# Graph attention, then multi-head attention over 64 graphs: the first batch's order, where weight sums are made, and the one-time checks

## The chip, the cores and the metric

The kernel runs on one core of a Trainium2 chip. The metric is the device time of one execution in microseconds; the median of several runs is compared. Engines are named as in the profile: PE is TensorE (PEld its weight loads), DVE is VectorE, ACT is ScalarE, POOL is GpSimd, SP is the engine that issues most DMAs.

## The reference

There are 64 graphs of 256 nodes with 512 features each, one adjacency matrix for all, and everything is float32.

```python
# layer 0
h = jnp.maximum(_layernorm(x, axis=-1), 0.0)
Wh = jnp.einsum('bnd,de->bne', h, W)
logits = (Wh @ a_src)[:, :, None] + (Wh @ a_dst)[:, None, :]
logits = jnp.where(logits >= 0, logits, 0.2 * logits)      # then -inf where adj == 0
x = x + jnp.einsum('bnm,bmd->bnd', jax.nn.softmax(logits, axis=-1), Wh)
# layer 1
h = jnp.maximum(_layernorm(x, axis=-1), 0.0)
q, k, v = (split_heads(h @ w.T + b) for w, b in ((Wq, bq), (Wk, bk), (Wv, bv)))   # 8 heads of 64
scores = jnp.einsum('bhqd,bhkd->bhqk', q, k) / 8.0         # then -inf where adj == 0
out = jnp.einsum('bhqk,bhkd->bhqd', jax.nn.softmax(scores, axis=-1), v)
x = x + out.transpose(0, 2, 1, 3).reshape(b, n, 512) @ Wo.T + bo
```

## The kernel before, in words

One batch (one graph, two tiles of 128 nodes) is one unit g. Each stage of a batch is a Python generator: `normalize0` (layer norm, ReLU, and the two row sums es and ed against W a_src and W a_dst, L514), `weights0` (exponentials of the logits on ACT, maximum on DVE, mask and sum, L540 to L545), `aggregate0` (h times the edge weights), `transform0` (times W, added to x), `normalize1`, `transpose1`, `project_qk`, `project_v`, `attention`, `scale`, `output`. The lists `first_half` and `second_half` say by hand, for every iteration i, which stage of which batch makes its next step, so a step that stands in the lists is issued at that place on every engine it uses. [...]

Big weight products are made by a seven-product scheme: a 2x2 block product with 7 instead of 8 block products. It needs sums of the left operand's quarters (`combine`: us for layer 0, hs for q, k and v, as for the output) and of the weights' quarters. `load_quarters` puts four quarters of a weight in slots B11, B21, B22 and T3; `combine_w` makes T1 and T2 (part 0), then overwrites T3 and writes T4N (part 1). T3 holds the upper right quarter until then. Before the change, all weight sums are on DVE (L158 to L162); `combine` is on DVE for batch 0 and on POOL for later ones (L170).

Batch 0 has no seven-product scheme in layer 0: it aggregates first (h times em, L575), then multiplies by W (L622) and adds to x with a scale by row (L628). While batch 0's first sums are made, `busy(12)` issues twelve transposes whose result nobody reads.

Layer 1's softmax is made without a maximum. `constants` is a generator that proves, on the chip, that this is safe: Gram matrices of each head's rows of Wq and Wk (`pgram`, L378, four groups), their squares and fourth powers (`squared`, L392), row sums of the absolute values (L408), squares of the bias rows (L424), of W a (L418) and of Wv (L438). If the check fails, a flag starts `general()`, a slower path, after the rest. `aside()` makes its next step; the prologue and, later, every fourth step of an iteration call it. The upper right quarter of each weight, which part 1 of `combine_w` overwrites, is loaded a second time for it:

```python
def load_b12(src, nm):
    b12 = work.tile([P, DC // 2, HD], F32, tag="b12", name=f"b12_{nm}", bufs=2)
    nc.gpsimd.dma_start(b12, quarter_of(src, 0, 1))
    return b12
```

`output_bias` makes bv @ Wo.T on PE (L333, eight products) and adds it to bo on DVE (L340); `bias_rows` then adds the row to x on POOL (L836).

[...]

Of the kernel before, what the change touches and what calls it, by code (L numbers as in the profile page):

```python
# [16 lines left out]
P = 128  # L17
# [11 lines left out]
def kernel(  # L29
# [102 lines left out]
    def bounded():  # L132
# [23 lines left out]
        def combine_w(wt, parts=(0, 1)):  # L156
            if 0 in parts:
                nc.vector.tensor_sub(wt[:, T1], wt[:, T3], wt[:, B11])  # L158
                nc.vector.tensor_sub(wt[:, T2], wt[:, B22], wt[:, T1])
            if 1 in parts:  # L160
                nc.vector.tensor_sub(wt[:, T3], wt[:, B22], wt[:, T3])
                nc.vector.tensor_sub(wt[:, T4N], wt[:, B21], wt[:, T2])  # L162
# [4 lines left out]
        def combine(a, s, g):  # L167


            engine = nc.gpsimd if g else nc.vector  # L170
            engine.tensor_tensor(s[:, 0], a(1, 0), a(1, 1), op=ALU.add)
            engine.tensor_tensor(s[:, 1], s[:, 0], a(0, 0), op=ALU.subtract)  # L172
            engine.tensor_tensor(s[:, 2], a(0, 0), a(1, 0), op=ALU.subtract)
            engine.tensor_tensor(s[:, 3], a(0, 1), s[:, 1], op=ALU.subtract)
# [61 lines left out]
        def load_b12(src, nm):  # L236

            b12 = work.tile([P, DC // 2, HD], F32, tag="b12", name=f"b12_{nm}", bufs=2)
            nc.gpsimd.dma_start(b12, quarter_of(src, 0, 1))
            return b12  # L240

# [12 lines left out]
        nc.gpsimd.dma_start(adj_sb, adj.rearrange("(c p) m -> p c m", p=P))  # L254
# [6 lines left out]
        wo_sb = load_quarters(woT, "wo_sb")  # L261
        for nm, src in (("bq", bq), ("bk", bk), ("bv", bv)):
            load_col(cols[nm], src)
# [5 lines left out]
        def node_weights():  # L269


# [5 lines left out]
            for c in range(DC):  # L277
                if c == DC // 2:
                    edge_mask()
                for j in range(2):  # L280
# [8 lines left out]
                    )  # L289
            return pas  # L290

        def edge_mask():
            adj_f = work.tile([P, NC, N], F32, tag="em", name="adj_f")
# [29 lines left out]
        def whole(wt, b12):  # L323
            return ((wt[:, B11], b12), (wt[:, B21], wt[:, B22]))

        def output_bias():

            wo_q = whole(wo_sb, load_b12(woT, "o"))
            yield
            pb = bank([P, D], "pbias")  # L330
            for j in range(2):
                for c in range(DC):
                    nc.tensor.matmul(  # L333
                        pb[:, j * HD : (j + 1) * HD],
                        cols["bv"][:, c : c + 1].to_broadcast([P, P]),
                        wo_q[c // 2][j][:, c % 2, :],
                        start=(c == 0),
                        stop=(c == DC - 1),
                    )
            nc.vector.tensor_add(bo_b, pb, bo_b)  # L340
            yield
# [13 lines left out]
        def constants():  # L355
# [8 lines left out]
            load_row(bo_b, bo)  # L364
            b12s = [load_b12(src, nm) for src, nm in ((wqT, "q"), (wkT, "k"))]
            yield
            for n in range(2):
                w_q = whole((wq_sb, wk_sb)[n], b12s[n])

                gm = work.tile([P, DC, DH], F32, tag="gram", name=f"gram_{n}", bufs=2)  # L370
                for pair in range(2):
# [13 lines left out]

                def squared(gm, power):
                    pgs = [bank([P, DC, DH], f"pgram{power}_{n}_{r}") for r in range(2)]
                    for e in range(DC):
                        for r in range(2):
                            half_p = slice(r * DH, (r + 1) * DH)  # L390
                            part = gm[half_p, e, :]
                            nc.tensor.matmul(pgs[r][half_p, e, :], part, part, start=True, stop=True)  # L392
                    return pgs

                pgs = squared(gm, 2)
                yield
                gm = work.tile([P, DC, DH], F32, tag="gram", name=f"gram2_{n}", bufs=2)
                for r in range(2):
                    half_p = slice(r * DH, (r + 1) * DH)
                    nc.scalar.copy(gm[half_p], pgs[r][half_p])  # L400
                yield
                pgs = squared(gm, 4)
# [10 lines left out]
            nc.vector.tensor_scalar(ok[:, 0 : 2 * DC], rows, 0.66, None, op0=ALU.is_le)  # L413
            junk = work.tile([P, D], F32, tag="junk", name="junk_b")
            sq = weights.tile([P, 4], F32, tag="sq", name="sq")
            nc.vector.memset(sq, 0.0)
            for j in range(2):
                nc.vector.scalar_tensor_tensor(  # L418
                    junk, wa[j], 1.0, wa[j], op0=ALU.mult, op1=ALU.mult, accum_out=sq[:, j : j + 1]
                )  # L420
            for j, src in enumerate((bq, bk)):
                row = work.tile([1, D], F32, tag="b12", name=f"brow_{j}", bufs=2)
                nc.gpsimd.dma_start(row, src.rearrange("(o e) -> o e", o=1))
                nc.vector.scalar_tensor_tensor(  # L424
                    junk[0:1, :], row, 1.0, row, op0=ALU.mult, op1=ALU.mult,
                    accum_out=sq[0:1, 2 + j : 3 + j],
                )
            nc.vector.tensor_scalar(ok[:, 2 * DC : 2 * DC + 2], sq[:, 0:2], 1.95, None, op0=ALU.is_le)
            nc.vector.tensor_scalar(ok[:, 2 * DC + 2 : 2 * DC + 4], sq[:, 2:4], 1.0, None, op0=ALU.is_le)
            yield  # L430
            big_v = weights.tile([P, 1], F32, tag="big_v", name="big_v")
            wv_q = whole(wv_sb, load_b12(wvT, "v"))
            svs = weights.tile([P, 2 * DC], F32, tag="svs", name="svs")
            for c in range(DC):
                for j in range(2):
                    sqv = work.tile([P, HD], F32, tag="junk", name=f"sqv_{c}_{j}")
                    wc = wv_q[c // 2][j][:, c % 2, :]
                    nc.vector.scalar_tensor_tensor(  # L438
                        sqv, wc, 1.0, wc, op0=ALU.mult, op1=ALU.mult,
                        accum_out=svs[:, 2 * c + j : 2 * c + j + 1],  # L440
                    )
                yield
            nc.vector.tensor_reduce(big_v, svs, AX.X, ALU.add)
            nc.vector.tensor_scalar(
                ok[:, 2 * DC + 4 : 2 * DC + 5], big_v, 1.0e8, None, op0=ALU.is_le
# [46 lines left out]
        def normalize0(g):  # L492
# [5 lines left out]
            stats = Stats(xt, h, f"0_{g}")  # L498
            for t in range(NT):
                stats.mean(t)  # L500
            yield
            for t in range(NT):
                stats.squares(t)
            nmr, rstd = stats.close()
            yield
# [60 lines left out]
        def aggregate0(g):  # L566
# [4 lines left out]
            for dp in range(0, DC, 2):  # L571
# [10 lines left out]
                if g == 0:  # L582
                    nc.scalar.copy(uT[:, dp : dp + 2, :], pu)
                else:
                    nc.vector.tensor_mul(
                        uT[:, dp : dp + 2, :], pu, edges[g][1].unsqueeze(1).to_broadcast([P, 2, N])
                    )
# [5 lines left out]
            scaled = edges.pop(g)[1]  # L593
            if g == 0:
                sums0[g] = uT, scaled
            else:
                sums0[g] = a, four_sums("us", g)
                combine(a, sums0[g][1], g)
            yield

# [12 lines left out]
        def transform0(g):  # L613

            a, s = sums0.pop(g)
            if g == 0:

                uT, rs = a, s
                for t in range(NT):
                    po = bank([P, D], f"po0_{g}_{t}")  # L620
                    for c in range(DC):
                        nc.tensor.matmul(  # L622
                            po, uT[:, c, t * P : (t + 1) * P], w_c[c // 2][:, c % 2, :],
                            start=(c == 0), stop=(c == DC - 1),
                        )
                        if c == 1:
                            yield
                    nc.vector.scalar_tensor_tensor(  # L628
                        xts[g][:, t, :], po, rs[:, t : t + 1], xts[g][:, t, :],
                        op0=ALU.mult, op1=ALU.add,  # L630
                    )
                    yield
                return
            yield from products(
                a, s, f"po0_{g}", partial(product_rows, w_sb), partial(add_to_rows, xts[g])
            )
# [27 lines left out]
        def transpose1(g):  # L664
# [13 lines left out]
            combine(a, lefts[g][1], g)  # L678
            yield

        def project_qk(g):
# [12 lines left out]
            def read(n, ps):  # L694
# [6 lines left out]
                elif n == 4:  # L701
# [6 lines left out]
                    return  # L708
                if held:
# [4 lines left out]
            yield from products(a, s, f"pqk_{g}", partial(product_cols, (wq_sb, wk_sb)), read)  # L714
# [124 lines left out]
        def scale(g):  # L839
# [15 lines left out]
            if s is not None:  # L855
                combine(a, s, g)
# [63 lines left out]
        bias = output_bias()  # L920
# [25 lines left out]
        S, E, W0, L1 = (normalize0, 0), (weights0, 0), (transform0, 0), (normalize1, 0)  # L946
        S_1, E_1, U_1, S_2 = (normalize0, 1), (weights0, 1), (aggregate0, 1), (normalize0, 2)
        steps(S, S, S)
        pas = node_weights()
        busy(12)  # L950
# [248 lines left out]
```

## Time and profile before

| what | us |
|---|---|
| median of 3 runs (2881.25 to 2884.21) | 2881.69 |
| profiled execution | 2883.55 |
| its span, first to last instruction | 2881.8 |
| PE busy in the span | 2857.6 |
| DVE, ACT, POOL busy | 2349.5, 1236.1, 1211.4 |

A group row of the profile names the line, the engine, the operation, then output and inputs by the program's names, and the busy time with the mean of one instruction in ns. A timeline row has the start in us, the length, engine, line and operation; in brackets stands how long the engine was idle before it, and what released it. "Lxyz" is the line in the kernel before. Matmuls in float32 appear as two instructions each.

### The profile page before, as it was taken

How to read it: one execution, taken by the hardware profiler on the slowest of the kernel's cores; microseconds unless marked ns; L12 is line 12 of the kernel's file. 1: busy time of each engine (PE TensorE's matmuls, PEld its weight loads, DVE VectorE, ACT ScalarE, POOL GpSimd, SP SyncE). 2: the span in 40 equal slices, each digit the busy share in tenths (PEclk: the TensorE clock that was granted, in tenths of full speed). 3: DMA queues.
4: the chain of work that ended last, by engine and by line, in shares of the span. 5: the costliest groups of instructions: out<-in, count | busy, mean ns of one | idle time of the engine just before them, and what ended most of it. 6: DMA issues, size and time to landing. Idle time of an engine off the chain costs nothing. (4 is left out here: it accounts for less than half of the span.)

```text
span 2881.8 us, 50781 instructions
## 1 busy us (share of the span) xinstructions
PE 2857.6 (99%) x19676; PEld 2471.1 (86%) x19676; DVE 2349.5 (82%) x3664; ACT 1236.1 (43%) x2986; POOL 1211.4 (42%) x1406
## 2 busy tenths in 40 slices
PE   8999999999999999999999999999999999999999
PEld 6788888888888888888888888888888888888886
DVE  7788888888888888888888888888888888888875
ACT  5443444434434444444344344444443443444432
POOL 2345344354454453443544534534435445345331
PEclk9999999999999999999999999999999999999999
DMA  4121222212212212222122122122221221221221
GB/s 143 20 40 33 40 35 33 45 31 37 45 30 38 38 34 41 33 35 45 30 37 45 30 38 37 35 41 33 35 45 30 38 45 30 38 36 35 34 40 29
DMA packets 82939, 111.89 MB, mean 39 GB/s; under 512 B 11652, under 2 KB 48516, under 8 KB 82694
## 3 DMA queue, kind: packets, MB, share of 16 engines
q1 hardware_dynamic: 82054, 107.00, 23.3%
q8 instruction: 158, 2.59, 0.4%
q0 software_dynamic: 640, 1.58, 0.2%
q14 instruction: 87, 0.71, 0.1%
HBM read 42.48 MB, written 33.55 MB: 26 GB/s over the span
## 5 line engine op out<-in xcount | busy, mean ns | idle before, releaser
L611 DVE TENSOR_TENSOR x<-po,x 128x1024 f32<-128x1024 f32 x875 | 595.0, 686 | 214.4 <-PE po L213 207.5
L485 POOL TENSOR_SCALAR ve<-ssq 128x2 f32<-128x2 f32 x128 | 24.6, 192 | 1090.5 <-ACT h L474 846.1
L758 DVE TENSOR_TENSOR ex<-ex,maskT 128x512 f32<-128x512 f32 x512 | 362.1, 748 | 0.0
L753 ACT ACTIVATE ex<-psc 128x512 f32<-128x512 f32 x512 | 257.8, 624 | 95.2 <-PE psc L745 95.2
L778 ACT COPY aT<-pav 128x512 f32<-128x512 f32 x128 | 75.0, 586 | 501.3 <-PE pav L770 470.0
L222 PEld LDWEIGHTS pqk<-hs,wq_sb 128*128 128x128 f32 x2048 | 268.3, 192 | 14.2 <-DVE hs L172 1.3
L222 PE MATMUL pqk<-hs,wq_sb 128*128 128x128 f32 x2048 | 270.2, 275 | 1.1 <-DVE hs L172 1.1
L222 PE MATMUL pqk<-hs,wk_sb 128*128 128x128 f32 x2048 | 270.5, 275 | 0.0
L213 PE MATMUL pv<-wv_sb,hs 128*128 128x256 f32 x1024 | 262.7, 379 | 0.5 <-DVE v L200 0.5
L514 DVE SCALAR_TENSOR_TENSOR junk<-wa,h 128x512 f32<-128x512 f32 x252 | 252.9, 1004 | 10.8
L213 PE MATMUL po<-wo_sb,as 128*128 128x256 f32 x992 | 255.4, 380 | 0.0
L222 PEld LDWEIGHTS pqk<-hs,wk_sb 128*128 128x128 f32 x2048 | 249.3, 192 | 0.0
L213 PE MATMUL po<-w_sb,us 128*128 128x256 f32 x1008 | 248.4, 379 | 0.0
L575 PE MATMUL pu<-em,h 128*128 128x256 f32 x1024 | 243.4, 381 | 1.9 <-DVE em L543 1.9
L745 PE MATMUL psc<-qk 64*128 64x256 f32 x2048 | 240.0, 384 | 1.8 <-DVE qk L207 1.8
L745 PEld LDWEIGHTS psc<-qk 64*128 64x128 f32 x2048 | 194.0, 188 | 48.3 <-issue 24.7
L770 PE MATMUL pav<-ex,v 128*64 128x256 f32 x2048 | 235.4, 382 | 0.0
L704 ACT ACTIVATE p<-pqk,bias 128x128 f32<-128x128 f32 x256 | 73.2, 369 | 353.2 <-PE pqk L222 353.2
L793 DVE RECIPROCAL rc<-psm 128x256 f32<-128x256 f32 x64 | 112.5, 1758 | 132.9 <-PE psm L785 132.9
L575 PEld LDWEIGHTS pu<-em,h 128*128 128x128 f32 x1024 | 195.6, 191 | 28.9 <-issue 2.0
L836 POOL TENSOR_TENSOR x<-x,bo_b 128x512 f32<-128x512 f32 x128 | 217.4, 1718 | 2.6 <-DVE bo_b L340 2.6
L770 PEld LDWEIGHTS pav<-ex,v 128*64 128x64 f32 x2048 | 141.4, 137 | 85.6 <-DVE x L611 19.2
(206 smaller groups left out, 5880.1 us busy)
## 6 DMA issues: line engine op xcount, KB each, us to landing
x<-in_x_dram SPq DMA_DIRECT2D x64, 512.0 KB, 5.6
out_dram<-x SPq DMA_DIRECT2D x128, 256.0 KB, 2.0
rb<-rc SPq DMA_DIRECT2D x496, 64.0 KB, 4.8
wq_sb<-in_L_gnn_Wq_dram SPq DMA_DIRECT2D x4, 256.0 KB, 9.5
wk_sb<-in_L_gnn_Wk_dram SPq DMA_DIRECT2D x4, 256.0 KB, 8.0
w_sb<-in_L_gnn_W_dram SPq DMA_DIRECT2D x4, 256.0 KB, 7.0
wv_sb<-in_L_gnn_Wv_dram SPq DMA_DIRECT2D x4, 256.0 KB, 8.8
wo_sb<-in_L_gnn_Wo_dram SPq DMA_DIRECT2D x4, 256.0 KB, 7.7
```

Of the source, the lines that this page charges most:

```text
L213: nc.tensor.matmul(dst[:, 0:HD], left[:, c, :], wt[:, slot, c, :], start=c == 0, stop=c == 1)
L222: nc.tensor.matmul(dst[:, at : at + P], wt[:, slot, c, e * P : (e + 1) * P], left[:, c, :], start=c == 0, stop=c == 1,)
L514: nc.vector.scalar_tensor_tensor(junk, (wa if g else pas)[a], 1.0, h[:, t, :], op0=ALU.mult, op1=ALU.mult, accum_out=dst[:, t : t + 1],)
L575: nc.tensor.matmul(pu[:, d, :], h[:, m, (dp + d) * P : (dp + d + 1) * P], em[:, m, :], start=(m == 0), stop=(m == NC - 1),)
L611: nc.vector.tensor_add(dst, src, dst)
L745: nc.tensor.matmul(psc[r][:, m, :], qk[rows, 2 + e % 2, m * P : (m + 1) * P], qk[rows, e % 2, :], start=True, stop=True,)
L753: nc.scalar.activation(ex[:, r, :, :], psc[r], AF.Exp, scale=SCALE)
L758: nc.vector.tensor_mul(ex[:, r, :, :], ex[:, r, :, :], maskT)
L770: nc.tensor.matmul(pav[r * DH : (r + 1) * DH, i, :], v[j][:, m, at : at + DH], pair[i][:, r, m, :], start=(m == 0), stop=(m == NC - 1),)
L778: nc.scalar.copy(aT[j], pav)
L793: nc.vector.reciprocal(rc, psm)
L836: nc.gpsimd.tensor_tensor(part, part, bo_b, op=ALU.add)
```

## The change

- Batch 0's layer 0 becomes a stage `layer0`: h is transposed, h @ W is made while the logits are made, and the edge weights are applied to the product. `aggregate0` and `transform0` lose their branch for g = 0.
- `combine_w` takes an engine: wk, w and wv are summed on POOL, wq and wo on DVE. `combine` is on POOL but for batch 0's hs.
- The Gram check stops at the square, with the bound on row sums 1.0 in place of 0.66 on fourth powers. The Gram matrices are made before part 1 of `combine_w` overwrites T3, so the second loads of quarters go. Squares of wv are made by ACT (`value_squares`), those of bq and bk from columns with one small product (`pq`).
- The output bias is made by four DVE steps and one product with a matrix of ones.
- The adjacency and bo are loaded from SP's queue. The mask is made after batch 0's es and ed.
- Batch 1's first layer norm takes its statistics from DVE's bn_stats instead of ACT.
- The prologue's order, iteration 0's lists, and the order of batch 0's seven q/k products are new (0, 2, 1, 3, ...), with product 2 held back for adding.

```diff
-        def combine_w(wt, parts=(0, 1)):
+        def combine_w(wt, engine, parts=(0, 1)):
...
+                    engine.tensor_tensor(wt[:, to], wt[:, a], wt[:, b], op=ALU.subtract)
-        def combine(a, s, g):
-            engine = nc.gpsimd if g else nc.vector
+        def combine(a, s, engine=nc.gpsimd):
...
-        nc.gpsimd.dma_start(adj_sb, adj.rearrange("(c p) m -> p c m", p=P))
+        nc.sync.dma_start(adj_sb, adj.rearrange("(c p) m -> p c m", p=P))
...
+        nc.sync.dma_start(bo_b, bass.AP(tensor=bo.tensor, offset=bo.offset, ap=[[0, P], [1, D]]))
...
                 if c == DC // 2:
-                    edge_mask()
+                    busy(4)
...
+                    if c >= DC // 2:
+                        busy(2)
...
-        def whole(wt, b12):
-            return ((wt[:, B11], b12), (wt[:, B21], wt[:, B22]))
+        def whole(wt):
+            return ((wt[:, B11], wt[:, T3]), (wt[:, B21], wt[:, B22]))
...
         def output_bias():
-            wo_q = whole(wo_sb, load_b12(woT, "o"))
-            yield
+            terms = work.tile([P, 2, HD], F32, tag="junk", name="terms")
+            for c in range(DC):
+                rows = wo_sb[:, B11 : T3 + 1 : T3 - B11] if c < 2 else wo_sb[:, B21 : B22 + 1]
+                part, bv_c = rows[:, :, c % 2, :], cols["bv"][:, c : c + 1]
+                if c == 0:
+                    nc.vector.tensor_scalar(terms, part, bv_c, None, op0=ALU.mult)
+                else:
+                    nc.vector.scalar_tensor_tensor(
+                        terms, part, bv_c, terms, op0=ALU.mult, op1=ALU.add
+                    )
             pb = bank([P, D], "pbias")
-            for j in range(2):
-                for c in range(DC):
-                    nc.tensor.matmul(
-                        pb[:, j * HD : (j + 1) * HD],
-                        cols["bv"][:, c : c + 1].to_broadcast([P, P]),
-                        wo_q[c // 2][j][:, c % 2, :],
...
+            nc.tensor.matmul(pb, ones, terms.rearrange("p j e -> p (j e)"), start=True, stop=True)
             nc.vector.tensor_add(bo_b, pb, bo_b)
+        def value_squares():
+            for n, slot in enumerate((B11, B21, B22, T3)):
+                junk = work.tile([P, DC // 2, HD], F32, tag="ex", name=f"junk_v_{n}", bufs=4)
+                nc.scalar.activation(
+                    junk, wv_sb[:, slot], AF.Square, accum_out=svs[:, n : n + 1]
+                )
...
+            if g == 1:
+                mv, rstd = norm_stats(xt, f"0_{g}", small)
...
+        def layer0(g):
+            h = nodes[g][0]
+            hT = big.tile([P, DC, TOK], F32, tag="uT", name="hT0")
+            for t in range(NT):
+                pt = bank([P, DC, P], f"pt0_{t}")
+                for c in range(DC):
+                    nc.tensor.transpose(pt[:, c, :], h[:, t, c * P : (c + 1) * P], ident)
+                nc.scalar.copy(hT[:, :, t * P : (t + 1) * P], pt)
+                yield
+            hw = big.tile([P, NT, D], F32, tag="qk0", name="hw")
+            for t in range(NT):
+                pw = bank([P, D], f"phw_{t}")
+                for c in range(DC):
+                    nc.tensor.matmul(
+                        pw, hT[:, c, t * P : (t + 1) * P], w_c[c // 2][:, c % 2, :],
+                        start=(c == 0), stop=(c == DC - 1),
+                    )
+                    if c == 1:
+                        yield
+                nc.scalar.copy(hw[:, t, :], pw)
+                yield
+            del nodes[g]
+            em, rs = edges.pop(g)
+            pos = [bank([P, D], f"po0_0_{t}") for t in range(NT)]
+            for m in range(NC):
+                for t in range(NT):
+                    nc.tensor.matmul(
+                        pos[t], em[:, m, t * P : (t + 1) * P], hw[:, m, :],
+                        start=(m == 0), stop=(m == NC - 1),
+                    )
+                    if m:
+                        part = xts[g][:, t, :]
+                        nc.vector.scalar_tensor_tensor(
+                            part, pos[t], rs[:, t : t + 1], part, op0=ALU.mult, op1=ALU.add
+                        )
+                        yield
+                if m == 0:
+                    yield
...
+            order = range(7) if g else (0, 2, 1, 3, 4, 5, 6)
...
         steps(S, S, S)
         pas = node_weights()
-        busy(12)
...
+        steps(S, L0, L0)
+        keep_wa(pas)
+        steps(L0, E)
+        edge_mask()
+        steps(L0, S_1, E, S_1, L0, L0, S_1, E, L0)
+        combine_w(wk_sb, nc.gpsimd, (0,))
+        combine_w(w_sb, nc.gpsimd, (0,))
+        combine_w(wq_sb, nc.vector, (0,))
+        prepare_biases()
+        steps(E_1, L0, L0, L1, E_1)
+        aside(6)
+        combine_w(wq_sb, nc.vector, (1,))
+        steps(L1, E_1, U_1, L1, U_1, X)
         aside(2)
...
+        combine_w(wk_sb, nc.gpsimd, (1,))
+        combine_w(w_sb, nc.gpsimd, (1,))
+        steps(X, X)
-        first = [(load, 3), K, K, E0, K, US, K, E0, K, K, K]
+        first = [(load, 3), K, D0, K, D0, K, US, K, D0, K, D0, K, E0, K, W, E0, W]
...
             if i == 0:
-                todo = first + second_half[:5] + [E0] + second_half[5:]
+                todo = first + [A, A, N0, E0] + second_half[6:]
...
+                if i == 0 and n == 6:
+                    value_squares()
                 if i == 0 and n == 8:
-                    combine_w(w_sb)
-                if i == 0 and n == len(first):
-                    combine_w(wv_sb)
+                    combine_w(wv_sb, nc.gpsimd)
                 if i == 1 and n == 6:
-                    next(bias)
+                    output_bias()
                     step(bias_rows, 0)
                 if i == 1 and n == 9:
-                    combine_w(wo_sb)
+                    combine_w(wo_sb, nc.vector)
```

## The prediction

> **What bounds the kernel now.** I read the table of engines first, then the span cut into five stretches at the PE instructions that matter here: the first q/k product of batch 0 (39.91 us), its last v product (79.83), the attention of batch 1 times its values (154.50), and the tail.
>
> ```profile
> PE 2857.6 (99%) x19676; PEld 2471.1 (86%) x19676; DVE 2349.5 (82%) x3664; ACT 1236.1 (43%) x2986; POOL 1211.4 (42%) x1406
> ```
> ```profile
> 0.00:39.91 39.91, 31.98 (x159) 20.52 (x159) 24.69 (x59) 24.76 (x57) 12.64 (x32) 0.96 0.78 252
> 39.91:79.83 39.92, 35.85 (x229) 31.86 (x228) 34.26 (x57) 18.76 (x45) 8.57 (x12) 0.96 0.02 6
> 79.83:154.50 74.67, 69.17 (x565) 60.70 (x565) 61.67 (x116) 30.90 (x95) 32.26 (x35) 0.95 0.14 22
> 154.50:2816.00 2661.50, 2661.50 (x18360) 2316.91 (x18360) 2192.28 (x3372) 1149.17 (x2762) 1148.65 (x1316) 1.00 0.24 37
> ```
> The columns are the stretch, its length, busy time of PE, PEld, DVE, ACT and POOL, PE clock, DMA share, GB/s. From 154.5 to 2816 us PE has no gap and a full clock. Nothing in the diff alters the order of instructions there beyond a few one-time checks, and the tail is the same. So the change is worth what it does before 154.5 us: PE idles 7.9, 4.1 and 5.5 us in the first three stretches, and runs below full clock in each. The waits and the timeline of the third stretch say why:
>
> ```profile
> 131.65 0.77 POOL L239 DMA_DIRECT2D b_v<-in_L_gnn_Wv_dram  x1
> ...
> 134.84 0.43 DVE L438 SCALAR_TENSOR_TENSOR sqv<-b_v 128x256 f32<-128x256 f32 x1 [2.73 <-DMA b_v<-in_L_gnn_Wv_dram]
> ...
> 138.10 0.45 PE L528 MATMUL pe<-ident,es 128*128 128x128 f32 x1 [4.12 <-DVE junk L514]
> ```
> DVE stands 2.73 us for a weight quarter asked for too late, the sums of batch 4 (L514) queue behind it, and PE waits. Stretches of 3.41 us before and after two other gaps:
>
> ```profile
> 17.44:20.85 3.41, 1.51 (x30) 1.27 (x25) 2.29 (x5) 3.38 (x7) 2.24 (x5) 0.98 1.08 356
> 20.85:24.26 3.41, 3.41 (x10) 2.74 (x9) 3.20 (x10) 0.59 (x1) 0.00 (x0) 0.52 1.07 359
> 54.99:58.40 3.41, 1.56 (x14) 1.31 (x14) 3.41 (x6) 0.00 (x0) 0.00 (x0) 0.98 0.00 0
> 58.40:61.81 3.41, 3.41 (x18) 2.77 (x18) 3.34 (x7) 2.17 (x4) 0.00 (x0) 0.52 0.00 0
> ```
> A stretch with PE under half busy is followed by one at half clock, which costs 1.7 us of work when PE is full. A gap near 1.8 us can thus cost twice its length.
>
> [...]
>
> ```profile
> 51.64 1.66 POOL L543 TENSOR_TENSOR em<-e,maskT 128x512 f32<-128x512 f32 x1 [8.05 <-DVE e L540]
> 52.20 1.65 DVE L159 TENSOR_TENSOR w_sb<-w_sb 128x512 f32<-128x512 f32 x1
> ```
> Alone, these take 1.27 (L836 at 86.8 us) and 0.69; against each other 1.66 and 1.65. I use 1.7 for a 512-wide DVE instruction against a saturated POOL.
>
> **Part A, start to first q/k product (39.91 before).** Up to 16.5 us nothing on the chain changes (x0, the two halves of W, eight L282, four L514). The adjacency DMA leaves POOL for SP and stands before x1 and the weights: 0.5 us of issue, 256 KB; but 512 KB of duplicate quarters (b_q, b_k) leave the same busy stretch, and its user now comes at 16.5, so I cost it at 0 (-0.7 to +0.5). PE now has work at once: eight transposes (0.11 each, 14.1 to 15.0), two copies by ACT (0.59 each), then h @ W, eight 128x512 products of 0.86 (L622: four issues in 1.72): 15.4 to 23.2, with the es transposes and the mask between. Beside it ACT makes four exponentials (0.36 each) and the mask copy until 19.9, DVE max, em and sum (0.69, 0.69, 0.42) until 21.1. So the wait that held PE at 18.2 to 20.0 is gone. Behind it the aggregation is four products, 3.4. Batch 0 costs PE 0.9 more in all than before (0.9 + 6.9 + 3.4 against 3.4 + 6.9), inside the former gap.
>
> What is late next is DVE. Batch 1 now takes its mean and variance there: two instructions that this trace has no row for, 0.42 to 0.75 each by the 512-wide DVE rows; I take 0.65, before ACT needs them. Its four L514 (21.3 on; 0.79 each free, 24.3 at the end) run against four subtractions for wk and w that are now on POOL: 1.7 for three, then 0.8, until 27.2. PE waits about 1.0 for them and ends the aggregation at 28.6. DVE then does the first two wq subtractions (1.4), biases (0.4), x0's two rows (0.75 each, until 31.0; before 33.75), then batch 1's logits until 32.8. PE covers that with three Gram groups (1.09 each, until 31.9), waits 1.0, aggregates batch 1 (3.4, until 36.7), transposes xn (ready at 36.2, stats 3.2 + POOL 1.2 + ACT 1.5 after x0), with the fourth Gram group between: first q/k product at 39.1. [...] I take **38.9: -1.0**, between -3.4 and +1. Two of the four Gram groups came from the third stretch.
>
> **Part B, batch 0 (39.92 before, of it 4.1 idle and 1.7 lost to the half clock; 34.1 of work, unchanged).** The wait on hs at 42 goes: a second product on hT stands before it. The wait on es stays. ACT now has batch 2's statistics (2.65) and four squares of wv (0.71 each) ahead of that batch's h, so h comes at 48.5 instead of behind the statistics. DVE's L514 then take 1.0 to 1.7 (POOL has us, 4 x 0.74, and four wv subtractions, 1.27 each, behind four of wk and w); the third ends near 52.6, and PE, done with six products at 50.5, waits **2.0** (1.1 to 4). The psc wait of 1.9 shrinks to **0.6**, as two w products stand before it. A new wait comes after psc: em and its sum for batch 2 stand on POOL behind the subtractions and behind DVE's max and a 1.22 us row addition: **1.2** (0 to 1.7). Clock 0.9 (half the chance of one half-rate window). Sum 34.1 + 4.7 = 38.8 against 39.9: **-1.1**, between -4 and +4.
>
> **Part C, batch 1 (74.67 before).** Gone: the b_v wait, 5.05 of PE idle at L528, the slow stretch after it (pqk pairs 1.70 for 0.89 each, and the rest: 2.0), and 0.4 at L392: -7.5. The eight sqv (0.5 each) and two brow (1.1) leave DVE, so its queue has no new user there. Two Gram groups, 1.08 + 1.09: -2.2. Two of four squarings, 0.61 and 1.0: -1.6. The small pq product: +0.15. The output bias: eight products, 3.46 (82.33 to 85.79), become one of 0.93; but it needs four DVE steps that stand behind four L514:
>
> ```profile
> 83.63 1.09 DVE L514 SCALAR_TENSOR_TENSOR junk<-wa,h 128x512 f32<-128x512 f32 x1
> 84.65 0.08 DVE L514 DVE_READ_ACCUMULATOR junk<-wa,h 128x1 f32 x1
> ```
> DVE is free for them only 4.9 after the last v product (84.73 against 79.83), and needs 0.48 + 3 x 0.72 = 2.65 more[...]. PE reaches the product 2.5 after that same point, with a squaring and one q/k product done; so a **new wait of 5.0** (3.5 to 6.5) and, by the rule above, 1.7 of half clock (0 to 2.5). Bias in all: 5.0 + 1.7 + 0.93 - 3.46 = +4.2. Sum of C: -7.5 - 2.2 - 1.6 + 0.15 + 4.2 = **-6.95**.
>
> The smaller moves cost nothing: batch 0's scale sums go to POOL, where every later batch has them; the bo load goes to SP's queue behind wo, some 50 us ahead of its use.
>
> **Sum:** -1.0 - 1.1 - 6.95 = -9.0. The profiled execution took 2883.55 (span 2881.8), 1.9 above the median of 2881.69; its own sum is 2874.5, and against the median I forecast **2872.7**.
>
> **Rivals.**
> *The waits eat it (0.18).* Batch 0's es wait at 4 (+2), its half-rate window for certain (+0.8), another at the psc or mask wait (+1.7), bias at the upper ends (+2.3): -2.2, 2879.5. For: DVE is 86% busy in that stretch. Against: work in front of each wait grew.
> *Cover holds (0.12).* No bias wait (DVE early by 5, -6.7): -15.7, 2866. Against: L514 of batch 3 cannot start before v is added up.
> *Slower (0.08): [...].* [...] I charge some 4. All of it on PE's path, with two more half-rate windows: +11.2 + 3.4 - 9.0 = +5.6, 2887.3; it decides once over 9.0 of those 14.6 reach PE. [...]
> *It doesn't do what it says.* If the shorter bound failed, the general path would run after everything; from the reference's weights the largest row sum is 0.86 against 1.0, so I leave it under 0.01.
>
> **Numbers.** Main case 0.62: 2872.7, with 2868 to 2876 its own range. Leaving out one in ten at each side gives 2867 to 2880. A measurement tells about 0.2% (5.8 us) from no change: faster by more 0.74, within 0.18, slower 0.08.
>
> **What would show it.** Right: PE without a gap from 15 to 25 us; no b_v wait, no idle near 134; a PE wait of some 5 us at the bias product on DVE, then half clock; one of about 2 at batch 2's es. Wrong: the bias product not waiting; a first q/k product after 41; PE gaps past 160 us.

## The result, and the profile after

| | before | after |
|---|---|---|
| median of 4 runs, us | 2881.57 (2881.25 to 2884.21) | 2874.43 (2873.44 to 2875.67) |
| profiled execution, us | 2883.55 | 2874.39 |
| its span | 2881.8 | 2872.3 |

The ratio is 0.9973, with a 95% interval of 0.9956 to 0.9991: faster by 0.27%, just over what a measurement of this kernel can tell.

The table of engines of the kernel after, and below it the span cut at the same PE instructions as before (first q/k product of batch 0, last v product, attention of batch 1 times its values, tail). The columns are the stretch, its length, busy time of PE, PEld, DVE, ACT and POOL, PE clock, DMA share, GB/s:

```profile
PE 2849.0 (99%) x19632; PEld 2462.8 (86%) x19632; DVE 2349.5 (82%) x3640; ACT 1235.0 (43%) x2984; POOL 1228.4 (43%) x1414
```
```profile
0.00:37.88 37.88, 32.09 (x222) 19.72 (x223) 29.06 (x64) 19.14 (x41) 14.59 (x28) 1.00 0.79 250
37.88:76.31 38.43, 34.08 (x230) 30.36 (x228) 33.52 (x46) 24.89 (x63) 20.44 (x23) 1.00 0.00 1
76.31:144.18 67.87, 62.43 (x457) 54.81 (x456) 58.27 (x99) 29.55 (x91) 35.23 (x36) 0.95 0.15 21
144.18:2806.00 2661.82, 2661.82 (x18362) 2317.09 (x18362) 2192.45 (x3370) 1149.22 (x2763) 1148.85 (x1316) 1.00 0.24 37
```

The first stretch went from 39.91 to 37.88 (-2.03), the second from 39.92 to 38.43 (-1.49), the third from 74.67 to 67.87 (-6.80). Together that is -10.32 at the attention of batch 1, and the attention of the last batch starts earlier by the same 10.3 (2856.78 against 2846.47): after 144 us nothing changed. The span is 9.5 shorter and not 10.3, because the last store ended 4.8 us after the last addition and not 3.8. In the profiled executions of the kernels below this end took 3.3 to 4.9, so a mark inside the kernel resolves finer than the total.

What PE waits for in the kernel after (total, times, longest):

```profile
PE pbias L337 <- DVE terms L333: 5.3, 1, 5.3
PE pe L525 <- DVE junk L511: 2.8, 2, 1.5
...
PE psc L771 <- DVE qk L206: 1.8, 1, 1.8
...
PE ps L556 <- POOL esum L542: 1.1, 1, 1.1
```

The wait of 4.12 near 134 us is gone. The largest is now the bias product's, and it is new. On DVE's timeline the four steps that make its operand stand behind four L511 (L514 in the kernel before) of batch 3; then PE's own rows:

```profile
80.11 1.09 DVE L511 SCALAR_TENSOR_TENSOR junk<-wa,h 128x512 f32<-128x512 f32 x1
...
81.24 0.49 DVE L331 TENSOR_SCALAR terms<-wo_sb,bv_c 128x512 f32<-128x512 f32 x1
81.77 2.33 DVE L333 SCALAR_TENSOR_TENSOR terms<-wo_sb,bv_c,terms 128x512 f32<-128x512 f32 x3
```
```profile
77.92 1.06 PE L221 MATMUL pqk<-hT,wk_sb 128*128 128x128 f32 x8
84.24 2.05 PE L337 MATMUL pbias<-terms,ones 128*128 128x512 f32 x2 [5.26 <-DVE terms L333]
86.08 1.92 PE L221 MATMUL pqk<-hs,wq_sb 128*128 128x128 f32 x8
```

A q/k product is recorded at 1.06 before the wait and at 1.92 after it, and the bias product at 2.05, where kernel a1 below, without the wait, has 1.02. The clock by stretches of 3.41 us:

```profile
78.17:81.58 3.41, 0.81 (x8) 0.61 (x6) 3.24 (x7) 2.43 (x12) 2.48 (x3) 1.00 0.00 0
81.58:84.99 3.41, 0.75 (x1) 0.50 (x2) 2.40 (x4) 2.03 (x10) 0.00 (x0) 0.50 0.00 0
84.99:88.40 3.41, 3.41 (x13) 2.66 (x12) 0.69 (x1) 0.00 (x0) 1.31 (x2) 0.50 0.00 0
88.40:91.81 3.41, 3.41 (x42) 3.22 (x41) 2.52 (x5) 1.59 (x5) 1.19 (x1) 1.00 0.00 0
```

Around the wait of 5.26 two stretches in a row have 0.81 and 0.75 of 3.41 busy, and the clock of the stretch behind each reads 0.50. PE is full only from 84.24 to 88.4 of these, which loses half of 4.2, 2.1 us. By this estimate from the rows above the wait's real price in this execution is 7.4.

It takes the place of the wait that is gone: PE idles 5.5 us in the third stretch before and 5.4 after. What was won there is busy time, 69.17 against 62.43, on 108 fewer PE instructions: two Gram groups and two squarings are gone from there, and eight bias products became one.

### The profile page after: what moved, and what is told of

The parts are those of the page before. It is cut to its first block, busy times and chain, and to the rows that moved or that the text cites. A ratio compares the mean times of both kernels' runs of the same rounds, so it can differ in the third digit from the quotient of the medians.

```text
span 2872.3 us, 50679 instructions
## 1 busy us (share of the span) xinstructions
PE 2849.0 (99%) x19632; PEld 2462.8 (86%) x19632; DVE 2349.5 (82%) x3640; ACT 1235.0 (43%) x2984; POOL 1228.4 (43%) x1414
## 5 line engine op out<-in xcount | busy, mean ns | idle before, releaser
L511 DVE SCALAR_TENSOR_TENSOR junk<-wa,h 128x512 f32<-128x512 f32 x252 | 258.6, 1026 | 11.6 <-ACT h L504 0.7
L796 PEld LDWEIGHTS pav<-ex,v 128*64 128x64 f32 x2048 | 141.2, 137 | 85.8 <-DVE x L643 19.9
L212 PEld LDWEIGHTS po<-w_sb,us 128*128 128x128 f32 x1008 | 191.5, 190 | 26.0
```

What stands on the lines that cost most here:

```text
L212: nc.tensor.matmul(dst[:, 0:HD], left[:, c, :], wt[:, slot, c, :], start=c == 0, stop=c == 1)
L511: nc.vector.scalar_tensor_tensor(junk, (wa if g else pas)[a], 1.0, h[:, t, :], op0=ALU.mult, op1=ALU.mult, accum_out=dst[:, t : t + 1],)
L796: nc.tensor.matmul(pav[r * DH : (r + 1) * DH, i, :], v[j][:, m, at : at + DH], pair[i][:, r, m, :], start=(m == 0), stop=(m == NC - 1),)
```

## The experiments

Ten kernels were run, each against the kernel before, whose medians in the three sessions were 2881.82, 2881.36 and 2881.65. "Start" is the start of batch 1's attention times values, 144.18 in the kernel after and 154.50 before.

| kernel | median, us | ratio to before (95%) | start |
|---|---|---|---|
| a1 bias product later | 2871.0 | 0.9964 (0.9952 to 0.9977) | 140.40 |
| a2 all weight sums on DVE | 2872.71 | 0.9967 (0.9956 to 0.9979) | 143.61 |
| a3 sums of wv later | 2871.24 | 0.9963 (0.9949 to 0.9977) | 140.00 |
| a4 before, without the late load of wv and its squares on DVE | 2873.52 | 0.9971 (0.996 to 0.9982) | 145.52 |
| b1 h @ W behind the logits | 2880.91 | 0.9997 (0.9989 to 1.0006) | 149.65 |
| b2 bias by eight PE products | 2870.51 | 0.9961 (0.9946 to 0.9977) | 140.44 |
| c1 three jobs later | 2864.89 | 0.9939 (0.9926 to 0.9953) | 134.95 |
| c2 the same and more | 2861.5 | 0.9929 (0.9916 to 0.9943) | 133.27 |
| d1 adjacency on GpSimd's queue | 2876.18 | 0.9981 (0.9973 to 0.9988) | 145.66 |
| d2 batch 1's statistics on ACT | 2878.37 | 0.9987 (0.998 to 0.9993) | 148.71 |

Starts and stretches are read from one profiled execution of each kernel. Counted from the kernel after, start and median moved alike to within 2.3 us, and to within 1.2 but for a4 and c2, so a difference of starts under about 1 us carries no argument alone.

The theory: the gain comes from the load that left the third stretch and from cover in the first; part of it is given back by one-time jobs that stand on DVE (or lengthen, from GpSimd, what it does: L203 took 1.75 for 0.68) in front of something that PE waits for. The rivals: DVE is late as such, whatever stands where; or the engine that makes the weight sums decides.

**a4: the late load and its squares**, taken out of the kernel before. ACT makes the squares of wv from the quarters already loaded, so the load and DVE's eight squares go. Four empty steps keep the later checks in their places; nothing else is changed.

```diff
-            wv_q = whole(wv_sb, load_b12(wvT, "v"))
...
-                    nc.vector.scalar_tensor_tensor(
-                        sqv, wc, 1.0, wc, op0=ALU.mult, op1=ALU.mult,
...
+                if i == 0 and n == 8:
+                    value_squares()
```

> The kernel before; only the squares of wv are changed: made by ACT in iteration 0 from the four slots ahead of the wv sums, so that the late second load of a wv quarter and the eight DVE squares of iterations 1 and 2 are gone. Theory (that load, through DVE's queue, made the whole PE gap at 134 us and the half clock after it): 5.05 + 2.0 us are won, batch 1's values product at 147.4 instead of 154.5, median 2874.5, as fast as the changed kernel. Rival (DVE stays late there for the other checks, 1.5 + 2.2 us of squares just ahead): only the 2.7 us of the load are won, 2878.8.

The three first stretches of that kernel:

```profile
0.00:38.57 38.57, 30.42 (x158) 19.48 (x159) 24.60 (x59) 24.76 (x57) 12.66 (x32) 1.00 0.82 261
38.57:76.80 38.23, 34.17 (x230) 30.65 (x229) 34.19 (x57) 20.93 (x53) 8.49 (x12) 1.00 0.02 6
76.80:145.52 68.72, 67.06 (x565) 58.76 (x564) 58.59 (x102) 30.89 (x95) 31.21 (x34) 1.00 0.15 20
```

The third stretch is 5.95 shorter than before, with the same 565 PE instructions: 3.84 less idle time, and 2.11 less busy time, as no half clock follows. What the load and the eight squares are worth apart is not shown. The start moved by 8.98 where 7.1 was expected. The other 3.0 lies in the first two stretches, where waits of about the old size still stand but the clock reads 1.00 and not 0.96: the two half-rate stretches of the kernel before did not occur in this run.

The traces suggest why; in the first stretch it cannot be the edit, which touches nothing there. In the kernel before half clock begins at 20.71, 58.26, 136.76 and 2881.06, which is 37.55, 78.50 and 2744.30 apart, or 11, 23 and 804 steps of 3.413. Each of the two early gaps fell inside one such step and left 1.51 and 1.56 us of it busy. As an estimate, with the same steps counted back from 2871.50, the one start of half clock in a4's trace, a4's first gap (1.76) left 1.65 of its step busy, and its second (1.84) lay across two steps, so that 2.15 of the emptier one was busy. The executions of one kernel differ in this too: in its 70 runs in the three sessions the kernel before has a mean clock from 0.997 to 0.999, while six of a4's seven have 1.000.

In the median this one edit gives as much as the whole change (0.9971 against 0.9973), but 3.0 of its 8.98 came with the clock of the first two stretches. Set against a4, the rest of the change gained and gave back about equal amounts.

**b1: the cover in the first stretch.**

```diff
-        steps(S, L0, L0)
+        steps(S)
         keep_wa(pas)
-        steps(L0, E)
+        steps(E)
         edge_mask()
-        steps(L0, S_1, E, S_1, L0, L0, S_1, E, L0)
+        steps(S_1, E, S_1, E, L0, L0, L0, L0, L0, L0, S_1, L0)
```

> The changed kernel, but batch 0's transposes and h @ W are issued behind its logits, not beside them. Theory (the product fills the gap in which PE waits for the logits): PE idles from about 14.5 us to 22, then has the transposes 0.9, h @ W 6.9 and the aggregation 3.4 in sequence. The first q/k product, 37.88 in the changed kernel, comes 5 to 6.5 us later, at 43 to 44.5, and all later marks with it; median about 2880. Rival (DVE's lateness sets the end of this stretch anyway, so PE's order does not matter): the first q/k product comes less than 2 us later, median 2875 to 2876.

PE's rows in that kernel:

```profile
20.58 1.02 PE L549 MATMUL ps<-ones,esum 128*128 128x1 f32 x4 [3.81 <-DVE esum L542]
21.46 1.95 PE L600 MATMUL pt<-ident,h 128*128 128x128 f32 x8
23.23 2.74 PE L607 MATMUL phw<-w_hT,hT 128*128 128x512 f32 x4
```

The last of them in the kernel after:

```profile
14.29 1.98 PE L607 MATMUL phw<-w_hT,hT 128*128 128x512 f32 x4 [0.24 <-ACT hT L601]
```

The first q/k product came at 43.75, 5.87 later than in the kernel after; the start 5.47 later. The theory's number holds: the product does fill the gap. But the gap's own length is not all of it. After the wait of 3.81 the eight transposes take 1.77 to the next row, where 0.9 is usual, and the first four instructions of h @ W 2.58, where 1.72 is. The profile's clock column reads 1.00 there, but the transposes took twice their usual time, as the q/k product above does at 0.50 (1.92 for 1.06); by these rows about 1.7 of the 5.87 is that. Without the cover the whole change is worth nothing (0.9997).

**d1 and d2: what else the first stretch's gain hung on.** It was 2.0 where 1.0 was forecast. d1 puts the adjacency's load back on GpSimd's queue, d2 makes batch 1's first statistics on ACT again.

```diff
# d1
-        nc.sync.dma_start(adj_sb, adj.rearrange("(c p) m -> p c m", p=P))
+        nc.gpsimd.dma_start(adj_sb, adj.rearrange("(c p) m -> p c m", p=P))
# d2
-            if g == 1:
+            if g == -1:
-        steps(L0, S_1, E, S_1, L0, L0, S_1, E, L0)
+        steps(L0, S_1, S_1, E, S_1, L0, L0, S_1, E, L0)
```

> The changed kernel with the adjacency loaded from GpSimd's queue again. Theory (in the first stage the second half of W lands earlier because the adjacency's 256 KB stand behind it on SP's queue, which is why the first stage won 2.0 us and not 1.0): the second half of W lands 1 to 1.5 us later, h @ W starts at about 15.4 in place of 14.3, the first q/k product at about 38.9, median about 1 us above the changed kernel. Rival (the second loads of two weight quarters, which are gone in both, made the difference): these marks stay within 0.4 us of the changed kernel's 14.3 and 37.88.

DVE's row at which the second half of W arrives, first in the kernel after, then in d1:

```profile
9.07 0.69 DVE L275 SCALAR_TENSOR_TENSOR junk_a<-pa,w_xn 128x512 f32<-128x512 f32 x1 [0.71 <-DMA w_xn<-in_L_gnn_W_dram]
```
```profile
10.48 0.69 DVE L275 SCALAR_TENSOR_TENSOR junk_a<-pa,w_xn 128x512 f32<-128x512 f32 x1 [1.79 <-DMA w_xn<-in_L_gnn_W_dram]
```

In d1 the adjacency's load is issued at 1.57, ahead of the second half of W (2.39), and is under way beside it (6.4 from issue to landing, W's 8.0); in the kernel after it is issued at 2.91, behind W (2.40, then 6.6 to landing). The edit changes the queue and the order at once, and which of the two counts is not shown. In the nine profiled kernels that load it behind W this row starts between 9.06 and 9.77; in the three that have it on GpSimd's queue at 10.43, 10.48 and 10.78. The rival, the absent second loads, is out. h @ W then starts at 15.68 in d1 for 14.29, and the first q/k product at 39.48 for 37.88, more than expected; h @ W starts anywhere from 13.91 to 15.13 in the kernels that leave this place alone, so a part of the 1.6 is scatter.

> The changed kernel with batch 1's first mean and variance made by ACT again (sums and squares, four instructions of about 0.66) in place of four of bn_stats and its aggregation on DVE. Theory (DVE's bn_stats pays because ACT is needed for exponentials and copies beside h @ W): batch 1's h is 2 us later, its four row sums on DVE are later by as much, PE's wait for them grows from 1.35 to over 2.5, and the first q/k product comes 1 to 2.5 us later than 37.88. Rival (DVE is the late engine there, so 1.7 us of work taken from it brings it forward): the first q/k product at 37 or earlier.

PE in d2:

```profile
29.10 0.47 PE L525 MATMUL pe<-ident,es 128*128 128x128 f32 x1 [3.01 <-DVE junk L511]
```

The first q/k product came at 41.85, 4.0 later, beyond the expected 2.5: the wait grew to 3.01, as expected, and a stretch at half clock (28.7 to 32.2, clock 0.50) followed, which was not. Of the 4.0, 0.6 is a later start of h @ W (14.90), which the edit does not touch, and about 1.5 is the half clock. ACT makes the statistics from 19.86 to 22.6, behind the exponentials and the mask copy, and DVE's row sums of batch 1 begin at 24.81 for 21.99. On DVE the statistics took 1.9 (15.40 to 17.30), at a time when it only waited for ACT.

**a2 and a3: the sums of weights.** a2 makes all of them on DVE; a3 leaves those of wv on GpSimd and issues them at the end of iteration 0's first half.

```diff
# a2
-        combine_w(wk_sb, nc.gpsimd, (0,))
+        combine_w(wk_sb, nc.vector, (0,))
...
-                    combine_w(wv_sb, nc.gpsimd)
+                    combine_w(wv_sb, nc.vector)
# a3
-                if i == 0 and n == 8:
+                if i == 0 and n == len(first):
                     combine_w(wv_sb, nc.gpsimd)
```

> The changed kernel with every weight sum on DVE, at the same places (wk, w, wv no longer on POOL). Theory [...]: the four L511 of batches 1 and 2 take 0.77 each instead of up to 1.63, L203 and L204 0.68 instead of 1.75; first q/k product within 0.7 us of 37.9, psc starts some 2 us earlier than 56.2, batch 1's values product at 142, median 2872. Rival (DVE is the scarce engine here and the 8 us of sums given back to it delay PE): values product at 147 or later, median 2877 or more.

> The changed kernel with the four wv sums on POOL moved from step 8 of iteration 0 to step 17, behind batch 2's em and its sum. Theory (these four sums hold up L511, L203, L204 and em of batch 2): es wait 1.5 to about 0.5, psc wait 1.8 to 0, esum wait 1.1 to 0: 4 us, batch 1's values product at 140.2, median 2870.4. Rival (the es wait is ACT's, whose four squares delay batch 2's h): es wait stays near 1.5 and at most 1.5 us are won.

The timeline of the kernel after where GpSimd makes the four wv differences, all engines:

```profile
48.24 6.73 POOL L163 TENSOR_TENSOR wv_sb<-wv_sb 128x512 f32<-128x512 f32 x4
...
50.54 1.63 DVE L511 SCALAR_TENSOR_TENSOR junk<-wa,h 128x512 f32<-128x512 f32 x1
...
50.56 0.32 PE L525 MATMUL pe<-ident,es 128*128 128x128 f32 x1 [1.48 <-DVE junk L511]
...
52.11 1.75 DVE L203 TENSOR_TENSOR qk<-qk,p 128x512 f32<-128x512 f32 x1
53.78 1.75 DVE L204 TENSOR_TENSOR qk<-s,p 128x512 f32<-128x512 f32 x1
```

L203 and L204 take 0.69 and 0.68 in a2, where GpSimd makes no differences. Beside GpSimd's each takes 1.75 here, and es and psc wait on PE for them. In a3 the second stretch is 34.54 long:

```profile
37.70:72.24 34.54, 33.94 (x230) 30.37 (x228) 30.29 (x46) 24.76 (x63) 19.97 (x23) 1.00 0.00 1
```

That is 3.9 less, nearly all of the 4.35 for which PE idles in that stretch of the kernel after (38.43 - 34.08). The wait at es fell from 1.48 to 0.60, and those at psc and esum are gone, so the rival (ACT's squares make the es wait) holds for 0.60 at most. The differences run without harm where nothing near them is awaited. In a2, made at the same early place by DVE itself, the stretch took 38.52, as in the kernel after: two waits of 1.87 and 1.15 at es and a stretch at half clock (50.7 to 54.1, clock 0.50) took the place of those at es, psc and esum. So the place of these sums costs 3.9, and in this stretch their engine makes no difference that can be told. In the first stretch it does: batch 0's em and its sum take 0.69 and 0.42 in a2, against 1.73 and 1.37 beside GpSimd's sums in the kernel after, and the first q/k product comes 1.1 earlier. The start is 0.57 earlier, so the rest was given back.

**a1 and b2: the output bias.** a1 issues its product ten steps later; the DVE steps stay. b2 makes it as eight products on PE from the loaded quarters, without the DVE steps.

```diff
# a1
+            yield
             pb = bank([P, D], "pbias")
...
                 if i == 1 and n == 6:
-                    output_bias()
-                    step(bias_rows, 0)
+                    bias = output_bias()
+                    next(bias)
+                if i == 1 and n == 16:
+                    next(bias)
+                    step(bias_rows, 0)
# b2
-            nc.tensor.matmul(pb, ones, terms.rearrange("p j e -> p (j e)"), start=True, stop=True)
+            for j in range(2):
+                for c in range(DC):
+                    nc.tensor.matmul(
+                        pb[:, j * HD : (j + 1) * HD],
+                        cols["bv"][:, c : c + 1].to_broadcast([P, P]),
+                        wo_q[c // 2][j][:, c % 2, :],
...
```

> The changed kernel; only the product of the output bias, its addition to bo and batch 0's bias rows stand later (at step 16 of iteration 1 instead of 6); the four DVE steps stay where they are. Theory (PE waits 5.26 us for those DVE steps and then runs two windows at half clock): wait and slow stretch are both gone, 5.3 + 2.0 = 7.3 us; batch 1's values product starts at 136.9 us instead of 144.18, median near 2867. Rival A (the half clock would have come anyway or costs nothing): only 5.3 us, 2869. Rival B (the DVE steps themselves delay the q/k additions behind them, and PE waits there for a free bank): under 3 us, 2872 or more.

> The changed kernel, but the output bias is made by eight products on PE from the loaded quarters of Wo (as in the kernel before, without its second load of a quarter), in the same place; the four DVE steps go. Theory (the bias product's wait for DVE costs its own length and the half-clock stretches behind it): the wait of 5.3 us, some 2.1 of half clock and one product of 0.93 give way to eight products of 3.46, so -4.8: attention times values of batch 1 starts at about 139.4 (144.18 in the changed kernel), median about 2869.5. Rival (DVE is late there whatever asks first, so the next PE instruction that needs it waits in place of the bias product): less than 2 us won, start at 142 or later, and a wait on DVE at another PE line in the same stretch.

b2: the third stretch is 4.26 shorter (67.87 to 63.61) with 2.53 more of PE work in it, its clock is 1.00, and the start is 3.74 earlier; the theory said 4.8. By the rows of the kernel after, the bias by DVE costs 5.26 + 2.1 + 0.93 - 3.46 = 4.8; b2 finds 4.26, as a new wait of 0.9 at pq takes a part.

a1 won 3.78 and not the expected 7.3. PE's rows later in that stretch show where the rest went:

```profile
93.87 0.35 PE L418 MATMUL pq<-sq,ones 128*128 128x2 f32 x2 [2.45 <-DVE junk_c L413]
```

The small product of the squared bias columns stands on PE while its two squares on DVE stand behind the differences of wo (2.61), the masking of two exponentials (2.52) and the bias addition. It had been covered by the stall ahead of it. Its 2.45 and another stretch at half clock (94.4 to 97.8, clock 0.50) came in place of the bias product's wait.

**c1 and c2: all of it.** c1 is a1 and a3 with pq three asides later. c2 also has the first sums of wk and W on DVE and the squares of wv three steps later.

```diff
# c1, beside a1 and a3
-            yield
+            for _ in range(3):
+                yield
             pq = bank([P, 2], "pq")
# c2, beside c1
-        combine_w(wk_sb, nc.gpsimd, (0,))
-        combine_w(w_sb, nc.gpsimd, (0,))
+        combine_w(wk_sb, nc.vector, (0,))
+        combine_w(w_sb, nc.vector, (0,))
-                if i == 0 and n == 6:
+                if i == 0 and n == 9:
                     value_squares()
```

> The changed kernel with three one-time jobs issued later: the bias product ten steps later in iteration 1, the small product pq three asides later, the sums of wv's quarters on GpSimd at the end of iteration 0's first half instead of its eighth step. Theory (each of these stood in front of an instruction that PE waits for; the gains of the two places add): -4.2 from the sums of wv and -7 from bias and pq, attention times values of batch 1 starts at about 133, median 2863 to 2864. Rival (the lateness of DVE moves on again to the next instruction that needs it): no more than the sums of wv and the bias alone gave, -4.2 - 3.8 = -8.0, start at 136 or later, median 2866.5 or above, with a PE wait of over 2 us on DVE left between 76 and 134 us.

> As the kernel with three jobs later, and besides: the first sums of wk's and W's quarters back on DVE [...], and the squares of wv on ACT three steps later. Theory: the first q/k product comes about 1.1 us earlier, as it did with all sums on DVE, and batch 2's h about 2.8 us earlier: attention times values of batch 1 starts at 131 to 132, median 1 to 2 us below the kernel with three jobs later. Rival [...]: within 0.7 us of it.

Two of PE's waits in c1, the longest of the third stretch and one in the tail, and the second and third stretches:

```profile
PE psc L774 <- DVE rc L822: 0.8, 1, 0.8
...
PE pv L212 <- DVE v L199: 0.5, 1, 0.5
```
```profile
38.98:73.53 34.55, 33.94 (x230) 30.36 (x228) 30.30 (x46) 24.76 (x63) 19.97 (x23) 1.00 0.00 1
73.53:134.95 61.42, 60.62 (x457) 53.45 (x456) 57.41 (x99) 29.50 (x91) 34.81 (x36) 1.00 0.16 23
```

The two gains add: -3.9 in the second stretch and -6.45 in the third. The start, 134.95, misses the expected 133 by 2, of which 1.1 is a first q/k product at 38.98 for 37.88, on a later start of h @ W (14.97 for 14.29). The rival's wait of over 2 us between 76 and 134 is not there; the longest is 0.8, at 97.9. So DVE is not late as such: the lateness was that of particular jobs. c2's first q/k product came at 37.63 and its start 1.7 earlier than c1's; the median is 3.4 lower, more than the 1 to 2 expected, and in the profiled executions 1.5 of that is the last store again. c2 is the fastest: 19.9 us below the kernel before, where the change brought 7.1.

## Why the prediction was right, and where its terms were off

- **The bound** was right: all of the difference lies before the attention of batch 1, and PE has no gap from there to the tail.
- **The sum**: -9.0 was forecast against the profiled execution, whose successor took 2874.39 where the sum said 2874.5. That it came so close is in part luck: the three parts moved the mark by 10.3, and the last store gave 1.0 back. The step that missed is the next one: 1.9 was taken off because the profiled run of before stood above its median. The profiled run of after stood on its median, and the forecast of 2872.7 was 1.7 too low.
- **Part A**, -1.0 said, -2.03 found. The term that failed is the adjacency's move to SP's queue, "I cost it at 0 (-0.7 to +0.5)": the second half of W came 1.36 earlier (10.43 to 9.07), and h @ W began at 14.29, not 15.4. d1 gave it back. The waits behind it were sized well: 1.35 at es for 1.0, 0.73 at the sum for 1.0. bn_stats took 0.69 and 0.66 for 0.65 assumed, with another 0.18 each for the aggregation. What the step did not name is that the edit is needed: d2 shows 4.0 of loss without it. It also charged batch 0's em and its sum at 0.69 and 0.42, and beside GpSimd's sums they took 1.73 and 1.37. And the size of the gain hangs on the clock: a4, with the old layer 0 and no half clock, has this stretch at 38.57, only 0.7 above the kernel after.
- **Part B**, -1.1 said, -1.49 found, but by errors that cancel. es waited 1.48 for 2.0, esum 1.1 for 1.2, psc 1.78 for 0.6: the two products ahead of psc did not help, since L203 and L204 each took 1.07 longer beside GpSimd's differences (1.75 for 0.68). The half-rate stretch, charged at 0.9 for half a chance, did not occur. That is the whole gain of this part: PE's idle time went from 4.1 to 4.35, so the new order won nothing here, and a4 has the stretch at 38.23 without it.
- **Part C**, -6.95 said, -6.80 found. The bias wait was 5.26 for 5.0; the half clock 2.1 for 1.7, since two stretches were at half rate and not one; b2 measures the bias edit at 4.26 for the 4.2 charged, with a new wait of 0.9 in it. The late load with its squares gave 5.95 in this stretch (a4). The 7.5 charged as gone counts two waits more, 1.08 at es and 0.38 at the squarings, which a4 still has and the kernel after has not. With them it is 7.41.
- **The rule for the clock**, half clock after a stretch under half busy, was the author's reading of two stretches of the kernel before (1.51 and 1.56 of 3.41 busy, 0.52 in the next). It held at the bias wait (0.81 and 0.75 busy, 0.50 behind each) but is too simple: in a1 a stretch with 1.51 busy (22.73 to 26.14), and in the kernel after one with 1.63 (54.28 to 57.69), were followed by full clock (1.00).
- **The rivals.** "Cover holds" failed at its first sentence: the bias product waited. Of what "The waits eat it" asked, only psc came (1.2 over the main case); es stayed below it, and no half-rate stretch fell into the second stretch. "Slower" put all of GpSimd's twelve subtractions (12 x 1.27, 15.2) on PE's path where the main case has 4, both the author's estimates. Some of it did reach PE: L203 took 1.75 beside them and 0.69 in a2, and the second stretch lost at most 3.9 (38.43 against 34.54 in a3), below the 9.0 at which it would have decided. Why DVE's instructions lengthen there is not shown. By a2 (38.52) the sums on GpSimd cost no more in that stretch than the same sums on DVE.

What stays open: what decides whether half clock follows a stretch in which PE is partly idle (1.51 of 3.41 busy was followed by it before and not in a1); and so how much of a4's 8.3 would come again with other places of the gaps. The third stretch shows 5.95 for the load and its squares.

## What to carry to other kernels

A one-time job costs what waits behind it, not its own time: four differences of weights cost 3.9 us at one place, where DVE was no better than GpSimd, and nothing that can be told nine steps later. When a wait is removed, look at the next instruction on that engine that needs the same late producer, and move both; in the third stretch the first alone brought 3.6 of the estimated 7.4 (a1), both brought 6.45 (c1). A change that gains as a whole can hide parts that lose: here one edit of many equalled the total in the median, and taking back the places of three others more than doubled it.

## What the hardware showed that was not expected

- In the kernel after a gap of 5.26 us lay across two stretches of 3.41 us with 0.81 and 0.75 busy, and the stretch behind each was at half clock (0.50); gaps of 1.48 and 1.78 in the same kernel were followed by none, and in d2 one of 3.01 by one. In b1 the same gap of 5.26 fell otherwise: two stretches were 2.02 and 0.00 busy, and only one at half clock followed (89.65 to 93.06, clock 0.50). Stretches with 0.81 (after) and 1.56 (before) of 3.41 busy were followed by half clock, one with 1.51 in a1 was not.
- The profile's clock column did not show a slow stretch in b1: it reads 1.00 from 21.46 to 24.8, while eight transposes took 1.77 for the usual 0.9 and four instructions of h @ W 2.58 for 1.72. The lengths of PE's rows show it.
- With the adjacency's 256 KB on GpSimd's queue, issued 0.8 us ahead of the second half of W (d1), W took 8.0 us from issue to landing and its first reader started at 10.48; with them on SP's queue, issued 0.5 us behind W (the kernel after), 6.6 and 9.07. No run separates the queue from the order.
- A 512-wide bn_stats in float32 took 0.66 to 0.69 us on DVE, as long as a 512-wide sum or difference there (0.68 to 0.69), and its aggregation 0.18.
